# A decoder layer in which every engine follows a written order: a new table of due times, and one context load at another place

## The chip, the core and the metric

The kernel runs on one core of a Trainium2 chip. Five engines work beside each other there: TensorE (PE in the profile, with its weight loads as PEld), VectorE (DVE), ScalarE (ACT), GpSimd (POOL), and SyncE (SP), which here issues most of the DMAs. Each takes its instructions in the order in which they were written, and waits where a semaphore isn't there yet. The metric is the device time of one execution in microseconds, as the median of several runs. Before the change it is 855.12 us (three runs, 855.03 to 855.30).

## What is computed

One decoder layer in float32 on 16 blocks of 128 tokens, 256 wide, in three parts, each with a LayerNorm before it and a residual sum behind it:

```python
x = x + attn(layernorm(x))           # 16 heads of 64: scores, softmax, values, output weights
x = x + xattn(layernorm(x), ctx)     # 16 heads of 16, keys and values from a context, masked keys
x = x + ffn(layernorm(x))            # 8 experts, 256 -> 512 -> 256, gelu, all summed, times a gate
```

In the two attentions each block meets only itself and its own context, so that the blocks can be worked on one after the other.

## The kernel before

**Two stages.** For the first half of the time the kernel works on both attentions of all 16 blocks, and for the second half on the experts, which the change does not touch. The first stage is a software pipeline of 16 slots. In slot s, block s goes through its own attention, block s-1 begins its cross attention, block s-2 ends it, block s-3 has its tokens transposed for the experts, and the queries, keys and values of later blocks are projected. The line `S0` of one slot to `S0` of the next is one turn of the pipeline.

**The order is a table.** A slot is cut into named steps. `slot()` (L1027) puts each step on a heap with a due time, `EXTRA + s * SLOT + DUE[name]`; `run_slots()` (L318) takes them off in the order of these times and writes their instructions. A step on TensorE mostly adds a second step that brings its result out of PSUM; this one has a due time of its own (`due()`, L299). The four compute engines are under a manual schedule, so the table fixes the order of instructions on each of them, and nothing else: no engine waits for a due time. A due time above `SLOT` lies in the following slot. `FIRST_DUE` holds the times of slot 0, `SECOND_DUE` and `LAST_DUE` some of slots 1, 14 and 15.

**The steps on TensorE**, in words, with their lines. A step that ends in `e`, or one that is named with an arrow here, brings a result out.

- `S0`, `S1` (L706): scores of the own attention, one half of the heads each, into one of two score tiles. `CS` (L841): scores of the cross attention, into both.
- `T1a1`, `T1a2`, `T1b1`, `T1b2` (L442): four transposes each of the own attention's softmax; a and b are the halves. `T2a1` to `T2b2`: the same for the cross attention. Out: `T1a1e` and so on. ACT copies T1 and T2a, DVE copies T2b.
- `SVa`, `SVb` (L731): values of the own attention -> `atT0`, `atT1` on DVE. `SO` (L751): its output weights -> `xsSO` on DVE.
- `CQ` (L819): queries of the cross attention -> `q2T` on DVE. `ck` (L768): its keys -> `cke`, `cke2` on ACT. `cvr` (L795): its value rows -> `cvre` on ACT. `CV` (L880): its values -> `at2T` on DVE. `CO` (L900): its output weights -> `xsCO` on DVE.
- `LN1`, `LNx`, `LN3` (L391): transposes of normalized tokens for the own attention (two blocks, in odd slots alone), for the cross attention and for the experts -> `LN1c`, `LNxc`, `LN3c` on ACT.
- `q1x`, `q1y`, `q2x`, `q2y` (L565), and the same with k and v: the projection of two blocks at once, by seven products in place of eight. `q1x` fills a PSUM bank with the products a and b, `q1y` another with f and e; `q2x` adds to a; `q2y` adds to f and e. Between them results are read out: `qu0`, `qc00` (ACT) and `qu1` (DVE) read the first bank, `qu2`, `qu3`, `qc1` and `qc0` (DVE) the second. So `q2y` can only be written when `qu2` and `qu3` have read.

**The steps on the other engines.** The softmax (L398) has four steps for each half of each attention: `max` on DVE (L406); `ex..a` and `ex..b` on ACT (L412), four exponentials each; `r..a`, `r..b`, reciprocals on DVE (L423); `mul..a`, `mul..b`, products on GpSimd (L427). The names of the cross attention begin with a c; `msk0` and `msk1` on DVE put its mask into the score tiles. `bn`, `bn3`, `root` on DVE find means and deviations, and `xn`, `xn3`, `xn1` (L382, DVE) normalize a block for the cross attention, for the experts and for the own attention. `ab1`, `ab2` (L395, GpSimd) add a bias to a block. `tf` (DVE) makes the sums of tokens for the projections of the next slots. `st0`, `mid`, `mid2`, `late`, `late2` (DVE) do the statistics of later blocks in a few slots.

**PSUM.** All tiles of TensorE but the scores come from one pool of four banks (`ps_mm`, L156); the score tiles take the other four (`ps_sc`, L159). A bank goes to the next tile when its last reader is done, and the tile framework puts the wait for that reader on the first instruction that writes the next tile.

**The context loads.** `contexts[g]` is the context of two blocks, 256 KB, in one of two buffers. SP issues the load of g + 2 from within a step of the second block of g.

Of the kernel before, what the change touches and what calls it, by code (L numbers as in the profile page):

```python
# [30 lines left out]
GB = 2  # L31
NG = B // GB
# [17 lines left out]
NROW = 528  # L50


SLOT = 26.98
EXTRA = 7.86
DUE = dict(
    S0=0.0, S1=1.0, T2a1=2.05, T2a2=2.49, T2a1e=2.69, ck=2.92, T2a2e=3.19, max0=3.47, v1x=3.79,
    cke=3.99, vu0=4.3, cke2=4.4, max1=4.61, v1y=4.66, q1x=5.52, ex0a=5.54, vu1=6.08, q1y=6.42,
    vu2=6.76, qu0=6.91, vu3=7.24, r0a=7.32, v2x=7.32, mul0a=7.39, vc00=7.4, ex0b=7.41, qu1=7.63,
    v2y=7.77, qu2=8.06, qu3=8.49, LNx=8.6, q2x=8.64, vc1=8.84, q2y=9.09, LNxc=9.1, ex1a=9.13,
    vc0=9.19, r0b=9.53, mul0b=9.81, qc1=10.19, cvr=10.21, qc00=10.51, qc0=10.54, r1a=10.98,  # L60
    T2b1=11.23, mul1a=11.26, cvre=11.31, ex1b=11.66, T2b2=11.66, T2b1e=11.86, CQ=12.1,
    T2b2e=12.46, T1a1=12.97, q2T=13.17, T1a2=13.4, r1b=13.51, xn1=13.6, T1a1e=13.6, mul1b=13.79,
    CS=13.93, st0=14.0, mid=14.0, late=14.0, T1a2e=14.1, ab1=14.9, CV=14.97, msk0=15.08,
    LN3=16.07, at2T=16.27, T1b1=16.29, LN3c=16.49, msk1=16.61, T1b2=16.73, T1b1e=16.93,
    LN1=17.16, T1b2e=17.43, SVa=17.47, cmax0=17.8, LN1c=17.93, SVb=18.38, tf=18.93, mid2=18.93,
    atT0=18.94, late2=18.94, cex0a=19.12, k1x=19.43, atT1=19.54, cmax1=20.14, k1y=20.33,
    cex0b=20.49, SO=21.23, cr0a=21.28, cmul0a=21.56, ku0=21.86, cr0b=22.14, cex1a=22.36,
    cmul0b=22.58, ku1=22.58, ku2=23.01, ku3=23.44, cex1b=23.74, cr1a=23.94, st1=24.0,
    cmul1a=24.3, k2x=24.68, xsSO=24.88, k2y=25.12, bn=25.28, kc00=25.32, cr1b=25.78, CO=26.03,
    cmul1b=26.06, kc1=26.22, kc0=26.57, xsCO=27.09, bn3=27.5, root=28.09, xn=34.27, ab2=34.3,  # L70
    xn3=37.78,
)


FIRST_DUE = dict(
    fk0=-11.4, fq0=-9.5, fk0e=-9.4, fq0e=-7.7, fk1=-7.2, norm1=-7.0, S0=-5.4, fk1e=-5.3,
    fq1=-4.4, max0=-4.0, cross=-3.0, ex0a=-2.7, fLN=-2.65, fq1e=-2.6, fv0=-2.3, fLNc=-1.4,
    r0a=-1.32, ex0b=-1.3, mul0a=-1.2, S1=-0.6, fv0e=0.1, r0b=0.15, mul0b=0.2, fab0=0.25,
    fab1=0.3, max1=0.4, fv1=0.41, ex1a=1.65, early0=1.7, early1=1.75, cvr=2.22, fv1e=3.0,
    r1a=3.1, mul1a=3.2, early2=3.3, early3=3.35, ex1b=3.6, q0=3.96, cvre=5.0, r1b=5.1,  # L80
    mul1b=5.2, q0e=5.3, early=5.4, k0=6.57, ke0=8.56, ws0=8.7, v0=9.18, xn1=10.44, T1a1=10.9,
    ve0=11.1, T1a2=11.34, T1a1e=11.54, T1b1=11.77, T1a2e=12.14, T1b2=12.21, LN1=12.64,
    T1b1e=12.74, LN1c=13.06, T1b2e=13.34, w0q=13.6, w0k=13.7, SVa=14.25, SVb=15.15, atT0=15.42,
    q1=17.2, atT1=17.21, wv0=17.3, q1e=17.6, k1=18.0, w1q=18.1, tf=18.2, SO=19.16, ke1=19.6,
    ws1=19.7, w1k=20.0, xsSO=22.81, bn=23.22, v1=23.47, root=24.79, xn=25.0, ck=25.2, ve1=25.39,
    q1x=26.9, cke=26.9, cke2=26.91, qu0=26.95, q1y=27.8, qu1=28.2, ab2=28.44, ab1=28.5,
    k1x=28.7, qu2=28.8, k1y=28.9, qu3=29.2, ku0=29.3, ku1=29.85, ku2=30.0, ku3=30.1, q2x=30.5,
    q2y=30.95, qc00=31.0, qc1=32.0, qc0=32.5, k2x=32.8, kc00=33.3, k2y=33.4, kc1=34.5, kc0=34.9,
# [7 lines left out]
        max0=1.2, max1=2.35, ex0a=3.3, cke=4.6, cke2=4.65, r0a=5.2, mul0a=5.4, vu0=5.9, ex0b=6.0,  # L96
        LNx=7.24, qu1=7.4, cvr=7.46, LNxc=7.6, ex1a=8.0, r0b=8.3, T2b1=8.33, mul0b=8.5,
        T2b2=8.77, T2b1e=8.85, CQ=9.2, T2b2e=9.3, cvre=9.5, ex1b=9.6, r1a=10.0, T1a1=10.1,
        mul1a=10.11, q2T=10.25, T1a2=10.55, CS=11.0, r1b=11.75, mul1b=11.85, CV=12.1,
        LN3=13.05, T1b1=13.3, T1b2=13.75,  # L100
    ),
}

# [11 lines left out]
def decoder_layer(  # L115
# [53 lines left out]
    def psum_mm(name):  # L169
        return ps_mm.tile([P, 512], F32, tag="mm", name=name)  # L170
# [51 lines left out]
    def context(g):  # L222
        c = work.tile([P, KD, GT], F32, tag="ctx", name=f"ctx{g}")
        nc.sync.dma_start(out=c, in_=ctxT[g])
        return c

    contexts = {0: context(0)}
# [55 lines left out]
    def urgent():  # L283

        return tc.high_priority()
# [5 lines left out]
    def at(name, f, *a):  # L291


        if now[0] is None:
            f(*a)
        else:
            heapq.heappush(events, (when(name), next(count), now[0], f, a))

    def due(name, f, *a):  # L299

        if now[0] is None:
            with urgent():
                f(*a)
        else:
            at(name, f, *a)

    def when(name):
# [3 lines left out]
        if s == 1 and name in SECOND_DUE:  # L311
            return EXTRA + SLOT + SECOND_DUE[name]
        d = LAST_DUE[s] if s in LAST_DUE and name in LAST_DUE[s] else DUE
        return EXTRA + s * SLOT + d[name]

# [446 lines left out]
    def cross_keys(b):  # L762
        kT = work.tile([P, C2, 2, T], F32, tag="k2T", name="k2T")
        g, i = b // GB, b % GB
        mm = psum_mm("mm_k2")[:, : C2 * T].rearrange("p (m t) -> p m t", m=C2)
        for m in range(C2):
            for k in range(KD):
                nc.tensor.matmul(  # L768
                    mm[:, m, :],
                    wx[:, 1, k, m * P : (m + 1) * P],  # L770
                    contexts[g][:, k, i * T : (i + 1) * T],
                    start=(k == 0),
                    stop=(k == KD - 1),
                )


        def out(m):
            for e in range(2):
                nc.scalar.activation(
                    kT[:, m, e, :],  # L780
                    mm[:, m, :],
                    AF.Identity,
                    bias=bkp[:, e, m : m + 1],
                    scale=par[:, e : e + 1],
                )

        due("cke", out, 0)
        due("cke2", out, 1)
        entry["k2T", b] = kT

    def cross_value_rows(b):
        g, i = b // GB, b % GB
        mm = psum_mm("mm_v2")
        for k in range(KD):
            nc.tensor.matmul(  # L795
                mm[:, :D],
                contexts[g][:, k, i * T : (i + 1) * T],
                wx_vo[:, 0, k, :],
                start=(k == 0),
                stop=(k == KD - 1),  # L800
            )
        due(
            "cvre",
            nc.scalar.copy,
            v2s[g % 2][:, i].rearrange("p (e w) -> p e w", e=2)[:, :, :D].rearrange(
                "p e (r t) -> p e r t", t=32
            )[:, :, :, :DH2],
            mm[:, :D].rearrange("p (r e d) -> p e r d", e=2, d=DH2),
        )
        if i == GB - 1 and g + 2 < NG:  # L810
            contexts[g + 2] = context(g + 2)

    def cross_queries(b):
        xnT2 = entry.pop(("xnT2", b))
# [212 lines left out]
    def slot(s):  # L1027


        for half in range(2):  # L1030
            at(f"S{half}", self_scores, s, half)
            at(f"SV{'ab'[half]}", self_values, s, half)
            for n in range(2):
                at(f"T1{'ab'[half]}{n + 1}", self_transposed, s, half, n)
                if s >= 2:
                    at(f"T2{'ab'[half]}{n + 1}", cross_transposed, s - 2, half, n)
        at("SO", self_output, s)
        at("cvr", cross_value_rows, s)
        at("ck", cross_keys, s)
        normalize_outputs(s, s - 2 if s >= 2 else None)  # L1040
        if s >= 1:
            at("LNx", cross_norm, s - 1)
            at("CQ", cross_queries, s - 1)
            at("CS", cross_scores, s - 1)
            at("CS", cross_softmax, s - 1)
        if s >= 2:
            at("CV", cross_values, s - 2)
            at("CO", cross_output, s - 2)
        if s >= 3:
            at("LN3", expert_norm, s - 3)  # L1050
        bs = [2, 3] if s == 0 else [s + 3, s + 4] if s % 2 and s + 4 < B else []
# [3 lines left out]
        if bs:  # L1055
            at("LN1", self_norm_transposed, bs)
        b0 = s + 2 - s % 2
# [18 lines left out]
        if s >= B - 2:  # L1076
            at("S0", load_w1, s - (B - 2), we1)
        for n, (s1, name, out) in enumerate(PRE_STEPS):
# [466 lines left out]
```

## Time and profile before

| | |
|---|---|
| runs without a profile | 855.12 us median |
| the profiled execution | 856.78 us |
| its span, first to last instruction | 855.0 us |
| PE busy | 846.0 us (99%), 5934 matmuls |
| DVE busy | 642.2 us (75%) |
| ACT busy | 474.6 us (56%) |
| POOL busy | 164.7 us (19%) |
| granted TensorE clock | 0.997 |

The steady slots run from about 100 to 400 us. There an even slot takes 26.88 to 26.89 us and an odd one 27.32 to 27.44 us, by the starts of `S0` in the chain of work that ended last; DVE is busy for 22 to 25 us of it and ACT for some 20. A record of the trace gives start and duration of one instruction. In a row of the timeline several instructions of one line are merged: start, duration from the first start to the last end, engine, line, operation, output and inputs, shapes, and how many. The difference of the starts of two rows of an engine is what the first of them took of it.

### The profile page before, as it was taken

The numbers are of one execution on the slowest core, as the hardware profiler recorded it, in microseconds if no ns is written. First come the engines' busy times: TensorE is split into PE (matmuls) and PEld (weight loads), VectorE is DVE, ScalarE is ACT, GpSimd is POOL, SyncE is SP. The second block draws the span as 40 slices with busy tenths as digits, with TensorE's granted clock in tenths as the row PEclk, the third lists the DMA queues.
The fourth block names the chain that finished last, engine by engine and source line by source line (L and its number), as shares of the span: only waits on it lengthen the run. The fifth ranks groups of instructions, "written<-read, shape, count | busy, mean of one in ns | idle before, by whom it ended". The sixth has DMA issues, their size and how long they took to land.

```text
span 855.0 us, 16389 instructions
## 1 busy us (share of the span) xinstructions
PE 846.0 (99%) x5934; PEld 721.8 (84%) x5934; DVE 642.2 (75%) x1694; ACT 474.6 (56%) x1723; POOL 164.7 (19%) x180
## 2 busy tenths in 40 slices
PE   8999999999999999999999999999999999999997
PEld 7899889888889889898775468888888888888886
DVE  4888998899888889888677497686557755676565
ACT  3567687776868668776685523343334333343332
POOL 4133242433423343332432000000000000000000
PEclk9999999999999999999999999999999999999999
DMA  8500000000000000001151100000000000000000
GB/s 238 148 13 2 2 14 2 15 1 2 13 2 14 1 2 14 2 2 51 56 196 46 50 1 0 1 13 13 1 0 1 26 1 0 1 13 13 2 0 26
DMA packets 18321, 21.32 MB, mean 25 GB/s; under 512 B 9584, under 2 KB 13696, under 8 KB 17600
## 3 DMA queue, kind: packets, MB, share of 16 engines
q1 hardware_dynamic: 17728, 19.93, 7.4%
q8 instruction: 47, 0.77, 0.4%
q0 software_dynamic: 368, 0.30, 0.2%
q14 instruction: 34, 0.28, 0.1%
q10 hardware_dynamic: 144, 0.04, 0.0%
HBM read 18.16 MB, written 2.10 MB: 24 GB/s over the span
## 4 chain that ended last, share of the span: by engine, by line
PE 93%; DVE 3%; ACT 2%; DMA 1%; issue 0%; POOLq 0%; DVEq 0%; SPq 0%; ACTq 0%
PE y L1279 20%; PE mm_qk L565 10%; PE tr_p L442 6%; PE mm_o L751 6%; PE he L1279 6%; PE hf L1279 6%; PE ha L1279 6%; PE mm_v L656 5%; PE sc L706 4%; PE po L731 3%; PE mm_h L1017 3%; PE hb L1279 3%; PE mm_qk L500 2%; PE y L1192 2%; PE po L880 2%; PE sc L841 2%
## 5 line engine op out<-in xcount | busy, mean ns | idle before, releaser
L412 ACT ACTIVATE cpr<-sc,nmax 128x128 f32<-128x128 f32 x256 | 90.5, 402 | 17.5 <-DVE nmax L406 14.0
L412 ACT ACTIVATE pr<-sc,nmax 128x128 f32<-128x128 f32 x256 | 93.0, 410 | 2.7 <-DVE nmax L406 2.7
L427 POOL TENSOR_TENSOR cpr<-cpr,rinv 128x512 f32<-128x512 f32 x64 | 65.5, 1040 | 126.4 <-DVE rinv L423 126.3
L1308 ACT ACTIVATE h<-u,colv 128x256 f32<-128x256 f32 x56 | 28.4, 508 | 99.4 <-DVE u L1295 97.5
L427 POOL TENSOR_TENSOR pr<-pr,rinv 128x512 f32<-128x512 f32 x64 | 67.1, 1049 | 62.8 <-DVE rinv L423 59.7
L406 DVE TENSOR_REDUCE nmax<-sc 128x8 f32<-128x1024 f32 x64 | 76.4, 1215 | 0.2 <-PE sc L706 0.2
L1309 DVE TENSOR_TENSOR c<-u,hf 128x256 f32<-128x256 f32 x56 | 23.5, 419 | 68.3 <-PE hf L1279 68.1
L1387 POOL TENSOR_TENSOR yT<-y,yu 128x256 f32<-128x256 f32 x1 | 0.7, 722 | 377.9 <-ACT y L1386 377.9
L1292 ACT COPY u<-ha 128x256 f32<-128x256 f32 x56 | 20.8, 372 | 83.5 <-PE ha L1279 83.5
L1279 PE MATMUL hf<-xt,w 128*128 128x256 f32 x224 | 66.7, 379 | 0.0
L1279 PE MATMUL ha<-xnT,w 128*128 128x256 f32 x224 | 66.6, 379 | 0.0
L1279 PE MATMUL y<-t,w 128*128 128x256 f32 x224 | 66.6, 380 | 0.0
L412 ACT ACTIVATION_READ_ACCUMULATOR pr<-sc,nmax 128x1 f32 x256 | 63.7, 249 | 0.0
L412 ACT ACTIVATION_READ_ACCUMULATOR cpr<-sc,nmax 128x1 f32 x256 | 61.9, 242 | 0.0
L751 PE MATMUL mm_o<-wo,atT 128*128 128x256 f32 x256 | 58.1, 380 | 0.3 <-DVE atT L324 0.3
L1279 PE MATMUL y<-h,w 128*128 128x256 f32 x224 | 57.6, 379 | 0.0
L751 PEld LDWEIGHTS mm_o<-wo,atT 128*128 128x128 f32 x256 | 47.6, 190 | 7.4 <-issue 1.0
L1279 PEld LDWEIGHTS ha<-xnT,w 128*128 128x128 f32 x224 | 42.6, 190 | 7.1 <-issue 1.2
L1279 PEld LDWEIGHTS hf<-xt,w 128*128 128x128 f32 x224 | 42.5, 190 | 5.9 <-DVE u L1294 0.2
L1279 PEld LDWEIGHTS y<-h,w 128*128 128x128 f32 x224 | 42.6, 190 | 5.8
L1279 PEld LDWEIGHTS y<-t,w 128*128 128x128 f32 x224 | 41.9, 190 | 6.2 <-issue 0.8
L395 POOL TENSOR_TENSOR xs<-xs,rowv 128x256 f32<-128x256 f32 x32 | 23.3, 740 | 115.2 <-DVE xn L382 115.2
(253 smaller groups left out, 2115.3 us busy)
## 6 DMA issues: line engine op xcount, KB each, us to landing
w<-in_w SPq DMA_DIRECT2D x8, 1024.0 KB, 5.2
ctx<-in_ctxT SPq DMA_DIRECT2D x8, 256.0 KB, 2.5
out_x<-ot SPq DMA_DIRECT2D x8, 256.0 KB, 2.1
xs<-in_x SPq DMA_DIRECT2D x3, 512.0 KB, 5.8
wk<-in_wk SPq DMA_DIRECT2D x2, 512.0 KB, 7.2
wq<-in_wq SPq DMA_DIRECT2D x2, 512.0 KB, 7.8
wv<-in_wv SPq DMA_DIRECT2D x2, 512.0 KB, 9.7
wo<-in_wo SPq DMA_DIRECT2D x1, 1024.0 KB, 7.7
```

The costliest lines, as they stand in the source:

```text
L406: nc.vector.tensor_reduce(w["nmax"], sc, AX.X, ALU.max, negate=True)
L412: nc.scalar.activation(w["pr"][:, i, :], sc[:, i, :], AF.Exp, bias=w["nmax"][:, i : i + 1], scale=1.0, accum_out=sums[:, j : j + 1],)
L427: nc.gpsimd.tensor_tensor(four, four, w["rinv", n].unsqueeze(2).broadcast_to([P, 4, T]), ALU.mult)
L442: nc.tensor.transpose(tr[:, j, :], w["pr"][:, 4 * n + j, :], ident)
L565: nc.tensor.matmul(out[:, q, :], paired[x, n][m - 1][:, q], paired[b0][m - 1], start=clears and q == 0, stop=True, skip_group_check=True,)
L656: nc.tensor.matmul(out, paired[b0][m - 1], paired["v", n][m - 1], start=clears, stop=True, skip_group_check=True,)
L706: nc.tensor.matmul(sc[:, j, c * T : (c + 1) * T], qT[r, c, :], kT[r, c, :], start=True, stop=True,)
L731: nc.tensor.matmul(po[j * DH1 : (j + 1) * DH1, c, :], v[:, h * DH1 : (h + 1) * DH1], prT[:, 4 * j + c, :], start=True, stop=True,)
L751: nc.tensor.matmul(mm[:, :D], atT[:, c, :], wo[:, c, :], start=(c == 0), stop=(c == C1 - 1))
L1017: nc.tensor.matmul(mm, w1q[p // (NP // QN)][:, i, k, p % (NP // QN)], xnT[:, k, :MT], start=(k == 0), stop=(k == KD - 1),)
L1279: nc.tensor.matmul(out, left[p // q][n - 1][:, p % q], rights[n - 1], **flags)
L1308: nc.scalar.activation(h[:, 1, 1], u[:, 3], AF.Gelu, bias=col(B1 + 2 * p + 1))
```

## The change

`DUE` is replaced, `SLOT` becomes 26.81, the entry of `LN3` leaves the table of slot 15, and the load of the next context is issued from `cross_keys` in place of `cross_value_rows`. No instruction is added or removed. With due times reduced to the slot in which they fall, the order changes as follows.

- TensorE: `ck` comes between `T2a1` and `T2a2`; `LNx` between `q2x` and `q2y`; `cvr` leaves the place behind `q2y` and comes between `T1a1` and `T1a2`; `LN1` comes behind `SVb` (before: ahead of `SVa`); `LN3` comes last in the slot, behind `CO` (before: behind `CV`).
- DVE: `xn` stays behind `vu3`; `r0a` moves from behind `xn` to behind `vc0`; `xn3` moves from behind `qc0` to between `msk0` and `at2T`; `T2b2e` comes ahead of `T2b1e`, with `r1b` and `q2T` between them; `msk1` and `cmax1` come behind both `atT`, and `tf` behind these; `qc1` moves from ahead of `qc0` to behind `ku3`, near the end of the slot; `cr1a` and `cr1b` move into the start of the next slot; `mid` and `mid2`, and `late` and `late2`, stand together ahead of `msk0`; `st0` of slots 3 to 5 comes behind `vc1`.
- ACT: `T2a2e` comes behind `cke`, `cke2` and `vu0`; `ex1b` ahead of `ex1a`; `qc00` ahead of `LNxc`; `cvre` behind `T1a2e`; `LN3c` last.
- GpSimd: `mul1b` ahead of `mul1a`; `ab2` from ahead of `mul0a` to behind `ab1`.

```diff
-SLOT = 26.98
+SLOT = 26.81
...
-    S0=0.0, S1=1.0, T2a1=2.05, T2a2=2.49, T2a1e=2.69, ck=2.92, T2a2e=3.19, max0=3.47, v1x=3.79,
-    cke=3.99, vu0=4.3, cke2=4.4, max1=4.61, v1y=4.66, q1x=5.52, ex0a=5.54, vu1=6.08, q1y=6.42,
-    vu2=6.76, qu0=6.91, vu3=7.24, r0a=7.32, v2x=7.32, mul0a=7.39, vc00=7.4, ex0b=7.41, qu1=7.63,
-    v2y=7.77, qu2=8.06, qu3=8.49, LNx=8.6, q2x=8.64, vc1=8.84, q2y=9.09, LNxc=9.1, ex1a=9.13,
-    vc0=9.19, r0b=9.53, mul0b=9.81, qc1=10.19, cvr=10.21, qc00=10.51, qc0=10.54, r1a=10.98,
-    T2b1=11.23, mul1a=11.26, cvre=11.31, ex1b=11.66, T2b2=11.66, T2b1e=11.86, CQ=12.1,
-    T2b2e=12.46, T1a1=12.97, q2T=13.17, T1a2=13.4, r1b=13.51, xn1=13.6, T1a1e=13.6, mul1b=13.79,
-    CS=13.93, st0=14.0, mid=14.0, late=14.0, T1a2e=14.1, ab1=14.9, CV=14.97, msk0=15.08,
-    LN3=16.07, at2T=16.27, T1b1=16.29, LN3c=16.49, msk1=16.61, T1b2=16.73, T1b1e=16.93,
-    LN1=17.16, T1b2e=17.43, SVa=17.47, cmax0=17.8, LN1c=17.93, SVb=18.38, tf=18.93, mid2=18.93,
-    atT0=18.94, late2=18.94, cex0a=19.12, k1x=19.43, atT1=19.54, cmax1=20.14, k1y=20.33,
-    cex0b=20.49, SO=21.23, cr0a=21.28, cmul0a=21.56, ku0=21.86, cr0b=22.14, cex1a=22.36,
-    cmul0b=22.58, ku1=22.58, ku2=23.01, ku3=23.44, cex1b=23.74, cr1a=23.94, st1=24.0,
-    cmul1a=24.3, k2x=24.68, xsSO=24.88, k2y=25.12, bn=25.28, kc00=25.32, cr1b=25.78, CO=26.03,
-    cmul1b=26.06, kc1=26.22, kc0=26.57, xsCO=27.09, bn3=27.5, root=28.09, xn=34.27, ab2=34.3,
-    xn3=37.78,
+    S0=0.0, S1=1.0, T2a1=2.05, ck=2.49, T2a1e=2.69, max0=3.34, T2a2=3.36, cke=3.56, cke2=3.61,
+    v1x=3.79, max1=4.48, v1y=4.66, vu0=4.86, T2a2e=5.21, q1x=5.52, vu1=5.62, ex0a=5.71,
+    vu2=6.05, q1y=6.42, vu3=6.48, qu0=7.08, v2x=7.32, v2y=7.76, qu1=7.8, vc00=7.96, qu2=8.23,
+    ex0b=8.31, q2x=8.62, qu3=8.66, vc0=9.01, LNx=9.07, q2y=9.29, r0a=9.35, vc1=9.48, mul0a=9.63,
+    qc00=9.68, st0=9.83, LNxc=10.18, T2b1=10.19, r0b=10.33, qc0=10.46, ex1b=10.48, T2b2=10.63,
+    mul0b=10.65, CQ=11.06, T2b2e=11.26, ex1a=11.85, T1a1=11.93, r1b=12.05, q2T=12.18,
+    mul1b=12.33, cvr=12.37, T2b1e=12.52, T1a1e=13.22, T1a2=13.24, r1a=13.42, xn1=13.55,
+    mid=13.6, late=13.6, mid2=13.65, late2=13.65, mul1a=13.7, CS=13.76, T1a2e=13.87, cvre=14.37,
+    CV=14.81, msk0=15.05, ab1=15.2, T1b1=15.91, T1b2=16.34, T1b1e=16.54, at2T=16.74, SVa=16.87,
+    T1b2e=17.04, cmax0=17.08, SVb=17.77, atT0=18.22, LN1=18.82, atT1=18.87, k1x=19.04,
+    LN1c=19.24, msk1=19.47, k1y=19.94, ku0=20.14, cex0a=20.64, cmax1=20.75, SO=20.84, tf=21.89,
+    cex0b=22.01, ku1=22.29, ku2=22.72, ku3=23.15, cex1a=23.38, qc1=23.5, st1=23.9, k2x=24.29,
+    xsSO=24.49, k2y=24.74, cex1b=24.76, cr0b=24.83, cr0a=24.96, bn=25.09, cmul0a=25.24,
+    CO=25.64, kc0=25.84, kc00=26.13, cmul0b=26.26, kc1=26.28, LN3=26.5, xsCO=26.7, LN3c=26.92,
+    cr1a=27.04, bn3=27.17, cmul1a=27.32, cr1b=27.67, root=27.8, cmul1b=28.34, xn=33.64,
+    xn3=43.05, ab2=43.41,
...
-        LN3=13.05, T1b1=13.3, T1b2=13.75,
+        T1b1=13.3, T1b2=13.75,
...
         due("cke2", out, 1)
+        if i == GB - 1 and g + 2 < NG:
+            contexts[g + 2] = context(g + 2)
...
-        if i == GB - 1 and g + 2 < NG:
-            contexts[g + 2] = context(g + 2)
```

## Prediction

> **What bounds the kernel now.** First the page: the busy times, and the chain that ended last.
>
> ```profile
> PE 846.0 (99%) x5934; PEld 721.8 (84%) x5934; DVE 642.2 (75%) x1694; ACT 474.6 (56%) x1723; POOL 164.7 (19%) x180
> PE 93%; DVE 3%; ACT 2%; DMA 1%; issue 0%; POOLq 0%; DVEq 0%; SPq 0%; ACTq 0%
> ```
>
> TensorE sets the end, so a step that moves on another engine counts only where TensorE waits for it. Then the windows of two steady slots (length, busy time of PE, PEld, DVE, ACT, POOL, clock, DMA):
>
> ```profile
> 291.43:318.31 26.88, 26.88 (x261) 24.16 (x260) 22.07 (x58) 19.73 (x87) 8.96 (x10) 1.00 0.01 2
> 318.31:345.63 27.32, 27.32 (x265) 24.60 (x264) 24.19 (x64) 20.34 (x88) 10.43 (x12) 1.00 0.03 11
> ```
>
> PE has no idle time there. The odd slot is longer by the four transposes of LN1, 4 x 0.109 us. But a busy PE can hide a short wait, so I went to the timeline and compared the starts of equal steps: q2x, q2y, cvr, later CQ, T1a (T1a1 with T1a2), CV, LN3, T1b, SV, k1x, and k2x, k2y.
>
> ```profile
> 300.20 0.61 PE L565 MATMUL mm_qk<-xnT,wq 128*128 128x128 f32 x4
> 300.77 0.71 PE L565 MATMUL mm_qk<-sums_q,wq 128*128 128x128 f32 x4
> 301.32 0.61 PE L565 MATMUL mm_qk<-xnT,sums_q 128*128 128x128 f32 x4
> ...
> 303.52 1.06 PE L819 MATMUL mm_q<-xnT,wx 128*128 128x128 f32 x8
> 304.41 1.04 PE L442 MATMUL tr_p<-ident,pr 128*128 128x128 f32 x8
> ...
> 306.45 1.08 PE L880 MATMUL po<-cprT,v 128*32 128x128 f32 x32
> 307.47 0.44 PE L391 MATMUL tr_x<-ident,xn 128*128 128x128 f32 x2
> 307.74 1.04 PE L442 MATMUL tr_p<-ident,pr 128*128 128x128 f32 x8
> 308.71 1.97 PE L731 MATMUL po<-prT,v 128*64 128x128 f32 x32
> 310.60 0.71 PE L565 MATMUL mm_qk<-xnT,wk 128*128 128x128 f32 x4
> ...
> 315.95 0.61 PE L565 MATMUL mm_qk<-xnT,wk 128*128 128x128 f32 x4
> 316.39 0.61 PE L565 MATMUL mm_qk<-sums_q,wk 128*128 128x128 f32 x4
> ```
>
> k2x takes 0.44 us (316.39 - 315.95), q2x 0.57, and the first half of q2y another 0.55 in place of 0.45: q2y waits, 0.22 us in all, in each of slots 1 to 13. It waits for qu3, and DVE shows when that ends (300.29 + 0.42 = 300.71; the matmul follows at 300.77, so a release takes 0.06 us):
>
> ```profile
> 300.29 0.42 DVE L324 TENSOR_TENSOR qT<-su,mm_qk 128x256 f32<-128x256 f32 x1
> ...
> 304.61 0.42 DVE L324 TENSOR_TENSOR q2T<-mm_q,bqk 128x256 f32<-128x256 f32 x1
> ```
>
> Behind a wait the weight load starts with the release and the matmul some 0.11 us later, as the lengthened row at 300.77 shows; before ordinary matmuls I add both. Before SV, whose weights wait for the array to be emptied anyway, I add the 0.06 alone. That one bank's reader can hold up the next tile is seen in slot 6, where SVa waits for the at2T that reads its bank (0.05 us over the usual change):
>
> ```profile
> 199.99 0.42 PEld L731 LDWEIGHTS po<-prT,v 128*64 128x64 f32 x8 [0.22 <-DVE at2T L324]
> ```
>
> Other waits in the first stage: SO for atT1, 0.54 us in slot 2 and 0.31 in slot 6, and about 0.6 in slot 1.
>
> **The sum, step by step, for a steady slot.**
>
> *q2y.* qu3 is late because qu1 to qu3 (1.40 us, 299.31 to 300.71) begin when ACT has done qu0, and qu0 stands behind ex0a. The new order starts ck 0.44 us earlier; cke then starts at 294.93, both pairs take 1.39 us (four such activations in one piece of the chain at 430.08), vu0 0.27, T2a2e 0.48 (starts of its pair), so ex0a starts at 297.07, not 297.26. On DVE cr1a and cr1b (0.12 us each) come in at the slot's start and r0a leaves; xn is then done at about 298.9, before qu0. So qu3 comes 0.19 us earlier and 0.03 of the wait is left. Between 0 and 0.12 I take 0.04: **-0.18**.
>
> *qc1 and cvr.* This is the largest term. q1y's bank is read by qc1, which now stands behind ku3, late in the slot. From q2y until then only three banks go round for T2b1, T2b2, CQ, T1a1, cvr, T1a2, CV, T1b and SV; before, qc0 and qc1 freed the fourth directly behind q2y. When cvr comes, the three hold T2b1 (T2b1e stands behind q2T), CQ, and T1a1 in the bank of T2b2. So cvr must wait for q2T. From the rows: CQ begins at x; T1a1 at x + 0.89 (304.41 - 303.52); its four transposes take 0.44, so cvr could start at x + 1.33. q2T ends at x + 1.51 (304.61 + 0.42 - 303.52); with 0.06 and 0.11 cvr starts at x + 1.68: **+0.35**. It can hardly be less, for q2T cannot start before CQ has ended; a late T2b2e only takes part of the same wait. Behind it the slack of T1a2, CS and CV grows, and nothing else is late.
>
> On this term stands a rule of the Trainium skill ("Perfetto Trace Analysis", Optimizing Tensor Performance, Matmuls): groups should rotate through different banks, so that bringing one out overlaps the next. It speaks against holding a bank for half a slot, but names no number; read literally, three banks still overlap a copy of 0.42 to 0.69 us with the groups behind it, which would make 0. The rows make 0.35, since only 0.44 us of transposes stand between CQ and cvr. I take the rows.
>
> *T2b2* takes the bank of q1x or of LNx. qc00, now ahead of ex1, ends at about 301.63 and LNxc at 301.84; T2b2's weight load is wanted at 301.9. Between 0 and 0.10: **+0.05**.
>
> *SVa.* It takes the next free bank, that of CV (at2T) or of T1b1 (T1b1e). With CV at c: msk0 starts at c + 0.11 and takes 1.20 (306.56 to at2T at 307.76), xn3 0.33, at2T 0.42, release 0.06: c + 2.12. Without LN3 between them SVa is wanted at c + 2.04 (1.02 for CV, 0.97 for T1b, 0.05 because the change of tiling now falls on T1b1). **+0.08**. If it is T1b1's bank, the ACT copy (308.38 + 0.59) ends later and it is +0.32; below 0.08 only if xn3 were free.
>
> *LN1 and LN3.* Transposes between SVb and k1x: k1x's first row takes 0.55 in place of 0.44 behind the tiled SVb, while LN3 behind the tiled CV takes 0.27 for two transposes of 0.109, that is 0.05 more. Odd slots gain 0.05. LN3 ahead of S0: behind transposes the second pair of matmuls of SVa comes after 0.15 us, behind CO's matmuls the second pair of S0 after 0.21: 0.05 gained, an estimate from SV. The Trainium skill ("TensorEngine Tiling (Array Packing)", Key Properties) says that a change of tiling mode drains TensorE: a slot has as many changes as before, so by the rule the sum is 0; by the rows the price depends on what comes next. I take the rows: **-0.07** as a mean of both kinds of slot.
>
> *Hidden.* cvre, T1a1e and T1a2e stand behind ex1a, but CV uses value rows of two slots earlier, and SVa comes 2 us behind them. atT1 ahead of msk1 and cmax1 gives SO over 0.9 us of slack, and cmax1 still ends over 1 us before cex1a is due on ACT. With cex1b later, S1's score tile is free 1.5 us before S1. In odd slots tf (0.93 us) behind cmax1 leaves ku3 0.6 us ahead of k2y; without that cover k2y would wait. cr1a and cr1b at the slot's start let cmul1b end at about 2.6 us of the slot, 7 us before T2b2. xn3 is used by LN3 10 us later, ab2 two slots later. A normalization that meets a GpSimd product waits for its end (1.13 us against 0.41, at 223.92); xn3 meets ab2 in odd slots alone, at its end, so this costs 0 to 0.2. The earlier context load changes nothing: its buffer is free only when cvr has read, SP's queue holds nothing else, a load lands in 2.5 us, and its reader is two slots away.
>
> Together: -0.18 + 0.35 + 0.05 + 0.08 - 0.07 = **+0.23 us a slot**, over slots 2 to 13: +2.8. The SO waits of slots 2 and 6 go: -0.85; mid and late, now in one piece of 12 small operations (2.3 us), push msk0 by 0.3 us there, without reaching SO. **+1.9 us.** The span of 855.0 becomes 856.9; the profiled execution (856.78) 858.7; on the median of 855.12 that is **857.0**.
>
> **Rivals.** *(1) The banks come free in time, and it gets faster.* Mechanism: SVa and cvr find a bank; it decides once the new bank waits stay below 0.25 us a slot (0.18 + 0.07). For it: before, qu3 is the only copy that PE waits for in most slots. Against: the dependence CQ, q2T, cvr above. At zero wait: -0.25 x 13 - 0.85 = -4.1, 851.0. *(2) SVa gets T1b1's bank,* or at2T is held up by xn3 behind ab2, so that it costs 0.32: +0.24 x 12 = +2.9, 859.9. For it: the two ends are within 0.25 us of each other. *(3) q2y still waits as before* because DVE, not ACT, is late (xn ends only 0.2 us before qu0): +0.18 x 13 = +2.3, 859.3.
>
> **How the numbers follow.** Less than 0.2% (1.7 us) is what a measurement of this kernel can't tell from no change. Forecast 0.56, of which 0.30 lies above 856.8, 0.23 within, 0.03 below 853.4; rival 1: 0.20 (0.17 faster, 0.03 same); rivals 2 and 3: 0.12 each, all slower. Faster 0.20, same 0.26, slower 0.54. The forecast's own range is 854.8 to 859.0; to leave out no more than 2 in 10 the range goes to 852.3 and 861.0.
>
> **What would show it.** cvr starting 1.68 us behind CQ with q2T as releaser; q2x at 0.45; SVa behind at2T; k1x at 0.44 in odd slots; slots of 27.1 us (even) and 27.5 (odd). Wrong if cvr follows T1a1 in 0.44 us, or if slots fall to 26.6 and 27.0.

## The result, and the profile after

The changed kernel takes **870.67 us** (median of 5 runs, 870.53 to 872.18), the kernel before 855.22 us beside it (5 runs, 855.03 to 855.52): a ratio of 1.0183, 95% interval 1.0171 to 1.0194. The forecast was 857.0 us, the range ended at 861.0. The direction was right, the size was not: +15.5 us in place of +1.9.

First the page of the kernel after: busy times, and the chain that ended last, by engine.

```profile
PE 853.0 (98%) x5934; PEld 721.5 (83%) x5934; DVE 654.8 (75%) x1694; ACT 476.2 (55%) x1723; POOL 163.8 (19%) x180
PE 82%; DVE 12%; ACT 3%; issue 1%; DMA 1%; POOL 0%; POOLq 0%; DVEq 0%; SPq 0%; ACTq 0%
```

Not one instruction was added (5934 on PE, 1694 on DVE, as before), yet DVE is busy for 12.6 us more (642.2 before) and PE for 7.0 us more (846.0). So some instructions take longer; the rows below show them waiting while they count as busy. And DVE's share of the chain went from 3% to 12%. Then the windows of an even and an odd steady slot (length; busy time of PE, PEld, DVE, ACT, POOL; clock; DMA):

```profile
298.53:326.25 27.72, 27.44 (x259) 24.24 (x259) 22.82 (x58) 19.86 (x88) 8.89 (x10) 1.00 0.01 2
326.25:354.37 28.12, 27.84 (x264) 24.63 (x263) 25.08 (x64) 20.46 (x89) 10.41 (x12) 1.00 0.03 11
```

Before, PE had no idle time in these slots (26.88 and 27.32 us); now 0.28 us of it show openly, and the slots are 0.84 and 0.80 us longer. The granted clock is 1.00 in both. The table has the slots from one `S0` to the next, from the matmul records of each profile. In the experiments, "root" puts `bn3` and `root` ahead of `cr1a` again, "qc1" puts `qc1` early again, and "split" moves `mid2` and `late2` back behind their first half.

| slot, us | before | after | e1: root | e2: qc1 | e3: both | e5: and split | e10: and the end |
|---|---|---|---|---|---|---|---|
| 2 | 27.20 | 28.56 | 28.37 | 27.74 | 27.60 | 26.75 | 26.74 |
| 6 | 27.24 | 29.41 | 28.90 | 28.44 | 28.11 | 27.28 | 27.28 |
| 8 (10, 12, 13 within 0.01) | 26.89 | 27.73 | 27.11 | 27.32 | 26.70 | 26.70 | 26.70 |
| 9 (7, 11 within 0.01) | 27.32 | 28.12 | 27.60 | 27.71 | 27.10 | 27.08 | 27.09 |
| 14 | 25.54 | 26.65 | 25.66 | 26.66 | 25.66 | 25.66 | 25.66 |
| 15 to the end | 430.14 | 432.64 | 437.15 | 432.65 | 437.29 | 437.48 | 430.52 |
| median | 855.2 | 870.67 | 867.36 | 864.19 | 860.84 | 859.81 | 852.31 |

The row of slot 8 stands for the even slots and that of slot 9 for the odd ones. So the loss has four places: the ten steady slots (3 to 5 and 7 to 13) +8.3 us, slots 2 and 6 +3.5, slot 14 +1.1, slot 15 and what follows +2.5; together 15.4, the difference of the medians. (The time up to the first `S0` is left out: it is 14.5 us in the profile of the kernel before and 12.6 to 13.2 us in the others. The granted clock was 0.55 from 7.2 to 11.0 us in that one execution, and 1.00 there in the kernel after.)

**The steady slot.** The starts of PE's rows in slot 10, an even one, say where its time went. The steps in the first column are taken from the start of the first to the start of what follows them; slots 8 and 12 give the same to 0.01 us. Differences named in the text are taken before rounding.

| us in slot 10 | forecast change | before | after | e10 |
|---|---|---|---|---|
| `v2x` and the first half of `v2y` | 0 | 0.87 | 1.44 | 0.87 |
| `q2x` and the first half of `q2y` | -0.18 | 1.12 | 0.99 | 0.94 |
| `T2b1`, `T2b2` | +0.05 | 0.89 | 0.87 | 0.87 |
| `CQ`, `T1a1`, `T1a2`, `cvr` | +0.35 | 2.73 | 3.07 | 2.73 |
| `T1b1`, `T1b2`, `CO`, `LN3` (waits of `SVa` and `S0`) | +0.08 - 0.05 | 2.20 | 2.26 | 2.20 |
| all other steps | 0 | 19.09 | 19.09 | 19.09 |

Four of these rows went about as forecast. The first did not: the timeline of the kernel after shows a wait that the prediction's sum does not have. `v2y` waits for `vu3`.

```profile
296.96 4.18 POOL L427 TENSOR_TENSOR cpr<-cpr,rinv 128x512 f32<-128x512 f32 x4 [9.31 <-DVE rinv L423]
...
298.53 2.06 PE L706 MATMUL sc<-kT,qT 64*128 64x128 f32 x32
...
299.56 0.60 DVE L370 TENSOR_SCALAR var<-mv 128x2 f32<-128x2 f32 x1
300.20 0.96 DVE L334 TENSOR_SCALAR root_t<-var 128x2 int32<-128x2 int32 x1
...
303.04 2.35 DVE L406 TENSOR_REDUCE nmax<-sc 128x8 f32<-128x1024 f32 x2
...
306.28 0.42 DVE L324 TENSOR_TENSOR v<-sv,mm_v 128x256 f32<-128x256 f32 x1
...
306.75 0.70 PE L656 MATMUL mm_v<-wv,sums_v 128*128 128x256 f32 x2 [0.28 <-DVE v L324]
```

The same operations in the kernel before:

```profile
290.52 1.04 POOL L427 TENSOR_TENSOR cpr<-cpr,rinv 128x512 f32<-128x512 f32 x1 [0.80 <-DVE rinv L423]
...
291.36 2.06 PE L706 MATMUL sc<-kT,qT 64*128 64x128 f32 x32
...
292.61 0.17 DVE L370 TENSOR_SCALAR var<-mv 128x2 f32<-128x2 f32 x1
292.81 0.17 DVE L334 TENSOR_SCALAR root_t<-var 128x2 int32<-128x2 int32 x1
...
294.86 2.35 DVE L406 TENSOR_REDUCE nmax<-sc 128x8 f32<-128x1024 f32 x2
```

The reader is to compare durations: two operations on two numbers per partition take 0.60 and 0.96 us after, 0.17 each before. Before, GpSimd's last product had ended (291.56) when `root` began. After, four products run one behind the other, from 296.96 to 301.14, and `root` falls into the last two. In the single records L370 ends 0.02 us behind the end of the third product (300.16 and 300.14), L334 0.02 us behind the fourth (301.16 and 301.14). `root` takes 1.2 us longer; `max0`, 3.50 us behind `S0` before (294.86 - 291.36; the window in the prediction begins 0.07 us later), comes 4.51 us behind it (303.04 - 298.53), and `v2y` waits for the sums behind it. That is what made DVE "busier".

The kind of operation matters too. In the kernel after, 26 such TENSOR_SCALAR operations on 128x2 elements (13 each of L370 and L334) begin while a GpSimd operation runs, and all 26 are held until it ends. In the same way 57 reciprocals, 62 batch-norm operations and 30 TENSOR_TENSOR sums of 128x256 elements begin beside GpSimd, and none of them is held. The Trainium skill ("SBUF — State Buffer", Who interferes with whom, with the section on SBUF's two sides) has the rule: VectorE and GpSimd share one pair of ports; an operation that takes the pair has it for its whole length, and the other engine's blocks until then. `tensor_scalar` is among the VectorE operations that the page names as able to take it. The ends and the kinds here agree with this.

### The profile page after: what moved, and what is told of

It is laid out like the page before. It is cut to its first block, busy times and chain, and to the rows that moved or that the text cites. A ratio compares the mean times of both kernels' runs of the same rounds, so it can differ in the third digit from the quotient of the medians.

```text
span 869.1 us, 16374 instructions
## 1 busy us (share of the span) xinstructions
PE 853.0 (98%) x5934; PEld 721.5 (83%) x5934; DVE 654.8 (75%) x1694; ACT 476.2 (55%) x1723; POOL 163.8 (19%) x180
## 4 chain that ended last, share of the span: by engine, by line
PE 82%; DVE 12%; ACT 3%; issue 1%; DMA 1%; POOL 0%; POOLq 0%; DVEq 0%; SPq 0%; ACTq 0%
PE y L1279 19%; PE mm_qk L565 8%; PE mm_o L751 6%; PE he L1279 6%; PE hf L1279 5%; PE ha L1279 5%; PE tr_p L442 5%; PE po L731 4%; PE mm_h L1017 3%; PE mm_v L656 3%; PE hb L1279 3%; DVE nmax L406 2%; PE y L1192 2%; PE mm_qk L500 2%; PE po L880 2%; PE sc L841 2%
## 5 line engine op out<-in xcount | busy, mean ns | idle before, releaser
L412 ACT ACTIVATION_READ_ACCUMULATOR cpr<-sc,nmax 128x1 f32 x256 | 66.1, 258 | 0.0
L412 ACT ACTIVATION_READ_ACCUMULATOR pr<-sc,nmax 128x1 f32 x256 | 59.3, 232 | 0.0
L324 ACT COPY prT<-tr_p 128x512 f32<-128x512 f32 x64 | 35.9, 601 | 36.9 <-PE tr_p L442 36.9
L324 DVE COPY_PREDICATED_SCALAR sc<-hidden_keys,masked 128x1024 f32 x30 | 38.5, 1282 | 15.3 <-PE sc L841 15.3
```

The costliest lines, as they stand in the source:

```text
L412: nc.scalar.activation(w["pr"][:, i, :], sc[:, i, :], AF.Exp, bias=w["nmax"][:, i : i + 1], scale=1.0, accum_out=sums[:, j : j + 1],)
```

## The experiments

Three of the first four kernels start from the kernel after, `e4` from the kernel before. Ratios, with their 95% intervals, are to the kernel before.

### The products beside root, the held bank

e1 and e2 each undo one part of the change, e3 both; e4 puts the cross reciprocals and products late in the kernel before.

```diff
 # e1: after
-bn3=27.17, root=27.8
+bn3=26.72, root=26.74
 # e2: after
-qc1=23.5
+qc1=10.45
 # e3: after, with both
 # e4: before
-cr1a=23.94, cmul1a=24.3, cr1b=25.78, cmul1b=26.06
+cr1a=27.2, cmul1a=27.3, cr1b=27.8, cmul1b=28.5
```

> After, with bn3 and root ahead of cr1a, so that GpSimd's products cmul1a and cmul1b start only when root is done. Theory P (the first small operations of root stand still while GpSimd multiplies, which makes max0 and then vu3 late): var and root_t take 0.17 us each again, the wait of v2y for vu3 (0.55 us a slot) goes in slots 2 to 13, and the time falls by 6 to 8 us, to some 863. Rival R (DVE is late because the two reciprocals and the bn steps stand ahead of max0): the same instructions stand there but for the reciprocals, 0.24 us; at most 0.25 us a slot comes back, 868 or more. Rival B (the bank of qc1 is behind everything): no change, 870.7.

Measured: 867.36 us (1.0146, 1.0129 to 1.0162), 3.3 less than after. The slots did as expected (0.62 and 0.52 us shorter, `v2y` without a wait), but slot 15 and what follows took 4.5 us more, which had not been expected; more of this below.

> After, with qc1 directly ahead of qc0, so that the fourth PSUM bank is free behind q2y. Theory B (as predicted, cvr waits for q2T and SVa for at2T because only three banks go round): the waits of T1a1 and cvr (0.32 us together) and of SVa (0.06 us) go, and with them the 1.2 and 1.5 us by which SVa waits in slots 2 and 6 behind mid and late; 870.7 - 12 x 0.38 - 2.7 = 863.4. If the waits come from the place of cvr between T1a1 and T1a2 alone, they stay: 870 to 871. The wait of v2y is not touched by it and stays at 0.55 us.

Measured: 864.19 us (1.0108, 1.0093 to 1.0123), 6.5 less: 0.40 us a slot, and 0.82 and 0.97 in slots 2 and 6. In the steady slots the held bank is as dear as forecast. In slots 2 and 6 less came back than the 1.2 and 1.5 that were expected: with the fourth bank free, `SVa` no longer waits there, but `SVb`, the next one, does (`SV` takes 2.66 us in slot 2 and 3.02 in slot 6, in place of 1.90).

> After, with both edits. If theories P and B are separate causes, the gains add: some 14 us less than after, 856 to 857, and a steady even slot of 26.8 to 26.9 us. If one hides the other, less than 11 us come back, 860 or more.

Measured: 860.84 us (1.0064, 1.0049 to 1.0080). The two gains add, 9.8 = 3.3 + 6.5, so they are separate causes; the 14 expected were not reached, since e1 had lost 4.5 of its gain at the end. The steady slots are now 0.19 and 0.22 us shorter than those of the kernel before; what keeps the kernel slower lies in slots 2 and 6 and at the end.

> Before, with cr1a, cmul1a, cr1b and cmul1b alone moved into the start of the next slot, around bn3 and root as after has them; no other step moves. Theory P: root's first operations stand still for the products, max0 to qu3 are late by about 1 us and v2y or q2y waits: 0.5 to 1.0 us a slot from slot 2 to 13, 861 to 867. Rival R: the reciprocals cost DVE 0.24 us a slot, q2y waits that much longer: 858. Rival B: no bank is held, so no change, 855.2.

Measured: 865.81 us (1.0122, 1.0105 to 1.0139). The same four positions cost the old order 10.7 us, in the range that was expected; its L370 and L334 take 0.60 and 0.96 us, and DVE is busy for 653.1 us in place of 642.2.

In e1 and e4 the reciprocals `cr1` on DVE move past `root` together with the products, so that these runs alone do not say which of the two delays it. e9 and e11 move or leave out the products alone.

```diff
 # e9: after, LAST_DUE[15] keeps the old values
-cmul1a=27.32, cmul1b=28.34
+cmul1a=31.5, cmul1b=31.6
 # e11: after
+            if x != "c" or h != 1 or now[0] == B - 1:
                 at(f"{x}mul{h}{q}", normalized, n)
```

> The kernel after (870.7 us) with the two GpSimd products cmul1a and cmul1b alone moved from the slot's start to behind max1; their reciprocals cr1a and cr1b stay ahead of root on DVE, and slot 15 keeps its order. Theory P (root's small operations stand still while a GpSimd product runs, so max0 and with it v2y are late): root's operations take 0.17 us again, v2y no longer waits, and the steady slots fall by 0.5 to 0.6 us to 27.1 to 27.2 us, the time to about 863 to 865 us. Rival Q (DVE is late because cr1a and cr1b, ahead of root, wait for the exponentials on ACT; the products do nothing): slots stay at 27.7 us, 870 us.

Measured: 870.36 us (1.0179, 1.0165 to 1.0193), slots of 27.72. This decides nothing: the table fixes only the order on each engine, and GpSimd has nothing else between the old place and the new one. Its order is the same, so the run is the kernel after once more.

> The kernel after (870.7 us) without the GpSimd products of the second cross half (cmul1a, cmul1b) in slots 1 to 14: those attention weights are not divided by their sums. DVE keeps its whole order, cr1a and cr1b ahead of root. Theory P (two of root's small operations stand still while a GpSimd product runs): root starts 1.03 us behind S0 as in the kernels after and e1_root_first, L370 and L334 take 0.17 us, v2y does not wait, and the steady slots fall by 0.5 to 0.6 us to 27.1 to 27.2 us (even). Rival Q (the order on DVE delays root): slots stay at 27.7 us.

Measured: 862.62 us (1.0085, 1.0068 to 1.0102), even slots of 27.11, odd ones of 27.60 to 27.61: those of e1 to 0.01 us. Its timeline, with DVE's order untouched:

```profile
295.27 2.06 PE L707 MATMUL sc<-kT,qT 64*128 64x128 f32 x32
...
296.30 0.17 DVE L370 TENSOR_SCALAR var<-mv 128x2 f32<-128x2 f32 x1
296.50 0.17 DVE L334 TENSOR_SCALAR root_t<-var 128x2 int32<-128x2 int32 x1
...
298.55 2.35 DVE L406 TENSOR_REDUCE nmax<-sc 128x8 f32<-128x1024 f32 x2
```

`root` begins 1.03 us behind `S0` here (296.30 - 295.27) and 1.03 us in the kernel after (299.56 - 298.53). So the order on DVE does not delay its start; the products beside it make it longer. The busy time of DVE agrees: 642.4 us in e11 and 643.2 in e1, but still 653.8 in e2, which leaves the products where they are. Theory P is shown.

Slot 6 of e11 is no part of this. It took 30.52 us in the profile, where e1 has 28.90. `SVa` waits 1.78 us for at2T in both, but behind this wait the granted clock fell in e11 alone (the clock is the third number from the end; e1 has 1.00 in the same window):

```profile
201.50:204.90 3.40, 3.33 (x32) 3.01 (x32) 1.84 (x3) 0.00 (x0) 0.00 (x0) 0.56 0.00 0
```

The other three executions of e11 took 862.46 to 862.76 us, the profiled one 864.21.

### The held bank in the old order

```diff
 # e8: before
-qc1=10.19
+qc1=23.5
```

> The kernel before with qc1 alone moved behind ku3 (one late reader of one PSUM bank). Theory (the held bank makes cvr or the transposes next to it wait for q2T in every slot, as the prediction had it): 0.30 to 0.40 us in 12 or 13 slots, 858.8 to 860.3 us. Rival (three banks are enough in the old order, where cvr comes before CQ): 855.1 us.

Measured: 863.53 us (1.0099, 1.0083 to 1.0114), +8.6: the theory's direction, about twice its size. Even slots grew by 0.54 us, odd ones by 0.53 to 0.76, slots 2 and 6 by 1.2. The timeline shows where: with one bank gone, `T2b2` gets the bank that `qc00` still has to read, on ACT behind the exponentials.

```profile
307.25 0.68 ACT L576 ACTIVATE qT<-mm_qk,colv 128x128 f32<-128x128 f32 x2
307.27 0.60 PE L442 MATMUL tr_p<-ident,cpr 128*128 128x128 f32 x4
...
308.08 0.63 PE L442 MATMUL tr_p<-ident,cpr 128*128 128x128 f32 x4 [0.21 <-ACT qT L576]
```

The four transposes at 307.27 should take 0.44 us; the next ones come 0.81 us later. That is 0.37 of the 0.54 us; the rest lies at `T1b`, whose eight transposes take 1.14 us to the start of `SVa` in place of 0.97. In the kernel after, `qc00` stands earlier on ACT, and the waits fall on `T1a1` and `cvr` (0.34 us together) and on `SVa` (0.06). What a held bank costs depends on whose turn the next one is.

### Slots 2 and 6, the end, and two versions that are faster

e5 is e3 with `mid2` and `late2` behind `cmax1`. e6 is e5 with a few positions changed in slots 14 and 15; e10 is e6 with the other reciprocals and products of slot 15 early as well. e7 is the kernel before with nothing but the new order at the slot's start, and `mid2` and `late2` behind `atT1`.

```diff
 # e5: e3
-mid2=13.65, late2=13.65
+mid2=21.85, late2=21.85
 # e6: e5, in LAST_DUE
+14: ku0=22.1
+15: ku0=22.1, cr1a=26.6, cr1b=26.62, cmul1a=26.64, cmul1b=26.66, bn3=27.5, root=28.09
 # e10: e6, in LAST_DUE
+15: cr0a=24.3, cmul0a=24.32, cr0b=24.34, cmul0b=24.36
 # e7: before
-T2a2=2.49, ck=2.92, T2a2e=3.19, cke=3.99, vu0=4.3, cke2=4.4, mid2=18.93, late2=18.94
+T2a2=3.36, ck=2.49, T2a2e=5.21, cke=3.56, vu0=4.86, cke2=3.61, mid2=19.9, late2=19.9
```

> The kernel of e3_both (root and qc1 put back: 860.8 us) with the second half of the normalizations mid and late (mid2, late2) moved from directly behind their first half to behind cmax1, so that they no longer stand ahead of msk0, xn3 and at2T in slots 2 and 6. Theory (the joined normalization holds at2T, so that SV waits for it): the waits of 1.04 us in slot 2 and 1.39 us in slot 6 shrink by the length of mid2 and late2 (about 1 us), and the time falls by 1.5 to 2.2 us to 858.6 to 859.3 us. Rival (the first half alone, two of whose operations stand still beside a GpSimd product, causes the wait): less than 0.6 us, above 860.2 us.

Measured: 859.81 us (1.0054, 1.0041 to 1.0067). Slots 2 and 6 became 0.85 and 0.83 us shorter, 1.7 us as expected; the median fell by 1.0 only, less than the 1.5 that was expected at least. Slots and median differ by 0.7 us, and the runs of e5 alone spread over 1.1 (859.19 to 860.25). In the kernel after, slot 6 looks so:

```profile
199.37 1.05 DVE L334 TENSOR_SCALAR root_t<-var 128x6 int32<-128x6 int32 x1
200.46 0.65 DVE L335 TENSOR_SCALAR root<-root_t 128x6 int32<-128x6 int32 x1
...
202.83 1.28 DVE L324 COPY_PREDICATED_SCALAR sc<-hidden_keys,masked 128x1024 f32 x1
...
204.34 0.42 DVE L324 TENSOR_TENSOR at2T<-po,colv 128x256 f32<-128x256 f32 x1
204.81 1.42 PE L731 MATMUL po<-prT,v 128*64 128x128 f32 x22 [1.48 <-DVE at2T L324]
```

`late` and `late2` run from 199.2 to 202.9 (two operations again lengthened, one by a product and one by the bias addition of GpSimd), then `msk0`, and only then `at2T`, which frees the bank for `SVa`: 1.48 us of open waiting.

> The kernel of e5_split with four positions of the last two slots changed: the hidden-layer copy ku0 behind cex0b in slots 14 and 15, and in slot 15 cr1a, cr1b, cmul1a, cmul1b ahead of xsCO, bn3 and root behind it. Theory (what is left of the loss sits at the end of the slots: 0.87 us of S1 in slot 15, and about 6.4 us of the transposes behind slot 15, which wait for the two products and then run at a granted clock of 0.68): the time falls by 6 to 8 us to 851 to 853 us, below the kernel before, because the steady slots are 0.2 us shorter than its own. Rival (the waits at the end only move to the expert layers): above 856 us.

Measured: 853.02 us (0.9977, 0.9967 to 0.9986), below the kernel before, as the theory had it. What most of this removed is seen in e3, behind slot 15: the transposes of the second score half wait for products whose reciprocals stand behind `root`, which stands behind CO's sum. The rows, then the windows of the same kernel around them (the clock is the third number from the end):

```profile
451.00 0.28 DVE L423 RECIPROCAL rinv<-sums 128x4 f32<-128x4 f32 x2
...
451.35 2.17 POOL L427 TENSOR_TENSOR cpr<-cpr,rinv 128x512 f32<-128x512 f32 x2 [3.54 <-DVE rinv L423]
...
452.53 0.66 PE L442 MATMUL tr_p<-ident,cpr 128*128 128x128 f32 x4 [3.52 <-POOL cpr L427]
```

```profile
448.00:452.00 4.00, 0.85 (x7) 0.42 (x4) 3.52 (x19) 1.59 (x4) 0.65 (x1) 1.00 0.27 115
452.00:457.30 5.30, 4.38 (x12) 2.34 (x12) 0.63 (x1) 1.17 (x2) 2.21 (x3) 0.68 0.01 3
457.30:465.00 7.70, 7.52 (x72) 4.86 (x72) 4.70 (x16) 1.92 (x4) 0.00 (x0) 1.00 0.00 1
```

Here PE's next work stands behind these transposes in the written order; 3.52 us are lost, and 1.4 more by the clock (last section). e1 has the same wait of 3.52 us. That is why it gave 3.3 us and not the 7.7 of its slots.

The kernel after, which has no such stall, still loses 2.5 us at this end: `S1` of slot 15 waits 0.65 us for `cex1b` (behind a `pre` copy that waited for PE ahead of `cex0a`), and the same transposes wait for products that begin when DVE has done `xsSO` and `xsCO`:

```profile
463.00 2.04 POOL L427 TENSOR_TENSOR cpr<-cpr,rinv 128x512 f32<-128x512 f32 x2 [0.48 <-PE tr_p L442]
...
464.10 0.66 PE L442 MATMUL tr_p<-ident,cpr 128*128 128x128 f32 x4 [0.37 <-POOL cpr L427]
...
465.10 0.66 PE L442 MATMUL tr_p<-ident,cpr 128*128 128x128 f32 x4 [0.34 <-POOL cpr L427]
```

> The kernel of e6_tail (853.0 us) with, in slot 15 alone, the reciprocals and products of the first score half (cr0a, cr0b, cmul0a, cmul0b) ahead of xsSO as well. Theory (the transposes behind slot 15 still wait 0.20 and 0.35 us because four products run one behind the other from 442.98 on, which begin only when SO's sum is done): those waits go and the time falls by about 0.7 us to 852.3 us. Rival (they then wait for bn3 or the copies instead): 853.0 us.

Measured: 852.31 us (0.9969, 0.9957 to 0.9981), the fastest of all. Its page, and two steady slots:

```profile
PE 842.5 (99%) x5934; PEld 721.5 (85%) x5934; DVE 642.2 (76%) x1694; ACT 473.3 (56%) x1723; POOL 163.8 (19%) x180
```

```profile
287.21:313.90 26.69, 26.69 (x260) 24.24 (x259) 21.93 (x58) 19.61 (x88) 8.88 (x10) 1.00 0.01 2
313.90:340.99 27.09, 27.09 (x264) 24.64 (x263) 24.44 (x64) 20.20 (x89) 10.38 (x12) 1.00 0.03 11
```

DVE is busy for 642.2 us again, as before the change. PE is busy for 3.5 us less than before, of which some 1.6 are the slow clock at the start of the profile of the kernel before.

> The kernel before with only the start of the slot in the new order (ck, cke, cke2 earlier, T2a2 and T2a2e and vu0 later) and mid2 and late2 behind atT1. Theory: q2y's wait of 0.18 us a slot goes (13 slots, 2.3 us) and the SO waits of slots 2 and 6 (0.85 us in all): 852 to 853 us. Rival (the wait of q2y is then set by xn and qu1 on DVE, not by ex0a on ACT): only the 0.85 us, 854.2 us.

Measured: 853.29 us (0.9980, 0.9971 to 0.9989). Slots 2 and 6 gave 0.91 us as expected, but the even steady slots only 0.08 (26.80), where 0.18 was forecast. The wait of `q2y` did go as the theory had it: `q2x` takes 0.45 us and the first half of `q2y` 0.50, together 0.17 less than before. But `T1a1` now comes 0.10 us later behind `CQ` (0.99 in place of 0.89); `CQ` itself was held up within its first product, by the bank that `qc00` still reads on ACT.

## Why the prediction was right or wrong, step by step

Right were the direction and the largest term that it had. The sum failed in three places that it had called hidden or had not looked at: they make some 13 of the 15.5 us.

- **cr1 and cmul1 at the slot's start ("Hidden"): the step that failed most.** The prediction asked when `cmul1b` would end, found it 7 us before its reader, and stopped. It did not ask what runs beside it. It had seen a normalization held up by a product (1.13 us for 0.41) and applied this to `xn3` and `ab2` alone. `cmul1b` did end 2.61 us into the slot, as forecast. Measured (e1, e11): `root` 1.2 us longer, `v2y` waiting, 0.62 us in even and 0.52 in odd slots, 1.0 in slot 14, 7.7 us in all, where the sum had 0. The prediction's own mark, slots of 27.1 and 27.5 us, failed at 27.72 and 28.12.
- **mid and late joined ("push msk0 by 0.3 us without reaching SO").** They did not reach `SO`, but they reached `SVa`, through the bank that `at2T` frees. Slots 2 and 6 were forecast at about 0.2 us less each (0.23 more, 0.43 less for `SO` on average) and grew by 1.36 and 2.17. The larger part is this step: from T1b to `SVa` it takes 1.20 us more in slot 2 and 1.56 in slot 6. The sum had the right link, msk0 to xn3 to at2T to SVa, in the step before, and did not carry the 0.3 us along it; and 0.3 was too small: the piece of 2.3 us took 3.7 in slot 6, as `root_t` and `root` were held up by GpSimd there too. e5 took 1.7 us back.
- **Slots 14 and 15** have fewer steps and other readers behind them; the steady sum was not redone for them. Slot 14 lost its 1.0 us at `v2y` (e1), and 2.5 us were lost at the end.
- **qc1 and cvr, +0.35: right,** mechanism and size. e2 gave 0.40 a slot, of which 0.06 is `SVa`; the rows of the kernel after are below: `cvr` comes 1.58 us behind CQ (forecast 1.68), when `q2T` has ended at 311.77. From CQ to T1a1, cvr and T1a2 they take 1.04, 0.54 and 0.96 us; in e2 the same steps take 0.89, 0.44 and 0.87, 0.34 us less. So 0.15 of the wait comes already ahead of `T1a1`, behind a late `T2b2e`, as the prediction allowed for. The rule of the page did warn of such a bank; the 0 that the prediction read out of it was wrong, the rows were right.
- **q2y, -0.18: right, but for the products.** `LNx` now follows `q2x` in 0.44 us, but q2y's first half still takes 0.54 in place of 0.45, so 0.12 of 0.22 went. This is because `root` makes all that follows on DVE late: where its delay is undone, q2y's first half takes 0.51 (e1) and 0.50 (e10), and in e10 and e7 0.17 went.
- **T2b2, +0.05:** T2b1 and T2b2 take 0.87 us together (309.38 to 310.25), no wait: 0. **SVa, +0.08: right,** behind at2T as forecast (the row at 316.49 below), 0.06.
- **LN1, LN3, -0.07:** LN1 gave 0.04 (odd slots grew by 0.80, even by 0.84); the second pair of `S0`'s matmuls behind LN3 still comes after 0.21 us and not after 0.15, so LN3 gave nothing. The 0 that the prediction had set beside its rows, from the rule on tiling modes, was nearer.
- **SO, -0.85:** those waits did go; the earlier wait for `SVa` stands in their place.

The rows of the kernel after for q2x to cvr, and for SVa (PE's starts give what each step took):

```profile
307.72 0.61 PE L565 MATMUL mm_qk<-xnT,wq 128*128 128x128 f32 x4
...
308.16 0.38 PE L391 MATMUL tr_x<-ident,xn 128*128 128x128 f32 x2
...
308.39 0.71 PE L565 MATMUL mm_qk<-sums_q,wq 128*128 128x128 f32 x4
308.93 0.61 PE L565 MATMUL mm_qk<-xnT,sums_q 128*128 128x128 f32 x4
309.38 1.04 PE L442 MATMUL tr_p<-ident,cpr 128*128 128x128 f32 x8
...
310.25 1.06 PE L819 MATMUL mm_q<-xnT,wx 128*128 128x128 f32 x8
...
311.29 0.63 PE L442 MATMUL tr_p<-ident,pr 128*128 128x128 f32 x4
311.35 0.42 DVE L324 TENSOR_TENSOR q2T<-mm_q,bqk 128x256 f32<-128x256 f32 x1
...
311.83 1.13 PE L797 MATMUL mm_v<-wx_vo,ctx 128*128 128x256 f32 x4
312.79 0.60 PE L442 MATMUL tr_p<-ident,pr 128*128 128x128 f32 x4
...
316.49 1.62 PEld L731 LDWEIGHTS po<-prT,v 128*64 128x64 f32 x30 [0.23 <-DVE at2T L324]
```

Rival (1), that the banks come free in time, did not hold: `cvr` and `SVa` wait for 0.40 us together. Rival (2) did not hold either, since `SVa` waits for at2T and for 0.06 us only. Rival (3) held in part, for a reason that it did not name. e10, in which the bank is free again and `root` is not held up, has steady slots of 26.69 and 27.09 us, near the 26.6 and 27.0 that the prediction gave for banks that are free in time. Of the 0.19 us that its even slots gain on the kernel before, 0.17 are q2y and 0.02 T2b (the table of slot 10). The prediction's sum counts q2y in 12 slots and rivals (1) and (3) in 13, a difference of 0.2 us.

## What to carry to other kernels

When a step is moved, ask not only who reads its result and when, but also what will run beside it: here two products of 1.04 us, hidden by every count of readers, made two tiny operations of another engine 3.5 and 5.6 times as long. The busy time of that engine grew by 12.6 us without one more instruction, and all but 1 us of this or less was gone where the products no longer met them (e1, e11). A busy time that grows while the count of instructions stays is the place to look first. And a steady sum holds for the steady slots alone: the slots with extra work and the last ones need sums of their own, because there a late step may have nothing behind which it can hide.

## What the hardware showed that was not expected

- DVE operations on 128x2 and 128x6 elements of the TENSOR_SCALAR kind take 0.60 to 1.05 us in place of 0.14 to 0.17 when they begin beside an operation of GpSimd, and end 0.02 to 0.03 us behind it. Not all are held: a reciprocal at 299.44 in the kernel after ran for 0.16 us in the middle of a product. And this kind is not alone: two SCALAR_TENSOR_TENSOR operations on 128x1 elements there (L349 at 74.15, L345 at 75.14) took 0.96 us each beside products, in place of 0.16 and 0.22.
- After a gap of 3.52 us PE became slower, though not at once: in e3 the four transposes at 452.53 still took 0.11 us each, the next four, from 453.58 on, about 0.21, and a 128x512 matmul 0.85 us where 0.43 is usual, until 456.8. The granted clock was 0.68 over 452.00 to 457.30 and 1.00 before and behind. From the second four transposes to the next CV it took 3.73 us, where the kernel after, at 1.00, takes 2.30 (465.10 to 467.40): so a wait of 3.5 us cost about 5. The Trainium skill ("TensorE: Matmul & The Clock Gate", Part 1) has TensorE at half rate after an idle window of about 3.4 us, for as long again; the times of e3 agree. But in the profile of e11 the clock fell to 0.56 behind a wait of only 1.78 us, and stayed at 1.00 behind the same wait in e1. So here the page's 3.4 us is no safe limit, and what decided between these two is open.
